# Four gathers, four transposes: one wait per chunk in place of one per transpose

## The chip, the cores and the metric

The kernel runs on one NeuronCore of one Trainium2 chip. The metric is the device time of one execution in microseconds (us), lower is better; where several executions were timed, their median is given. All data is float32.

## What is computed

The reference is the forward pass of a recommendation model. For each of 16384 rows of a batch there are 69 item numbers (fields) and one label number. Each number selects a row of 96 floats from an embedding table of 100001 rows.

```python
u  = emb[batch_user]                         # 16384 x 69 x 96
ql = emb[batch_label[:, 0]]                  # 16384 x 96
z  = concatenate([q, u, q - u, q * u])       # q: ql, repeated for every field
h  = dice(z @ W1 + b1, a1) @ W2 + b2
att = h @ W3 + b3                            # one number per row and field
pre = where(batch_user < ITEM_NUM, u * att, 0)
pooled = einsum('gf,bfe->bge', window, pre)  # 10 groups of fields
x  = concatenate([pooled, ql])
h  = dice(bn(x @ Wf1 + bf1), af1)            # then Wf2, then Wf3
```

`dice(x)` is `(alpha * (1 - p) + p) * x` with `p = sigmoid(x)`. So there are 16384 x 69 = 1.13 million row fetches for the fields, and for each fetched row a small network whose result weights the row in a sum.

## The kernel before, in words

**Tiling.** The batch is cut into 32 blocks of 512 rows (`NBLK`, `BLK`). Of a block, the first 64 fields make 64 chunks of 8 rows x 64 fields, and each of the 5 remaining fields makes a chunk of 512 rows; that is 69 chunks of 512 fetched rows. Two chunks are a pair: 1104 pairs (`NPAIR`), the unit of all loops.

**Fetching.** `fetch(i)` (L298) allots three tiles for pair i: `u` (128 partitions x 8 x 96, from a pool of 14), and the transposed `uT` and `quT`. For each of the two chunks it issues four gathers (L307, which calls `gather`, L226; the profile shows them under L227). A gather is an indirect DMA that GpSimd (POOL) issues: it takes 128 row numbers, one per partition, from the SBUF tile `rows`, and brings 128 table rows of 384 bytes into `u`. After each gather `fetch` records the TensorE transpose of what it brought (L308), into a quarter of the PSUM tile `ptr`. When all four quarters are there, VectorE multiplies `ptr` by the transposed label rows into `quT` (L311, L318), and ScalarE copies `ptr` into `uT` (L319).

**The other stages**, each on an earlier pair: `seed` (L278, a matmul that clears a PSUM bank, and a ScalarE copy into it), `hidden` (L326 the first layer on TensorE; L328 and L329 sigmoid and scaling on ScalarE; L330 the product on VectorE), `attend_rows` (L337, once per four pairs), `spread` (once per four pairs: four transposes L353, then on VectorE L356, and L359, which builds the weights `rw` from two SBUF tiles, `R` and `w`), `pool` (L376, the weighted sum, up to eight matmuls per pair, and L385, its way out), and for the last fields of a block `attend_tail` (L346, L347). Per block there is a top network: `top1` (L406, two halves in four parts each; then L410 on VectorE, L411 and L412 on ScalarE, and L413 on VectorE, a product of two SBUF tiles), `top2` (L420, L421 to L423, and L424, again a product of two SBUF tiles) and `top3` (L429, L431).

**Order.** The order on each engine is written out by hand, in the loop L474 to L507. Step i issues `seed(i-1)`, `pool(i-8)`, every fourth step `attend_rows` or `spread`, `hidden(i-2)`, `fetch(i)`, and after that what the `plan` holds for this step: loads, the gathers of the next block's labels (128 in all, also L227), and one part of the top network. Each engine works through its own queue in this order; the framework adds the semaphore waits that the data needs. A gather into a `u` tile waits for the last matmul of `pool` that read the same tile 14 pairs earlier, and for the gather that used the same one of eight DMA semaphores before.

**Waits in `fetch`.** In the built program [...]a separate event-semaphore instruction with up to two waits stands ahead of it in its engine's queue. The first transpose of a chunk waits for its gather in such an instruction, and for ScalarE (which has to have read the `ptr` tile's earlier contents) in its own. The second, third and fourth each wait for their own gather. In the built program each of the eight transposes of a pair also raises TensorE's semaphore when it is done; VectorE waits for the value of the fourth.

Of the kernel before, what the change touches and what calls it, by code (L numbers as in the profile page):

```python
# [32 lines left out]
I32 = mybir.dt.int32  # L33
AF = mybir.ActivationFunctionType
ALU = mybir.AluOpType
PSUM = bass.MemoryType.PSUM

P = 128
# [25 lines left out]
def rec_kernel(  # L64
# [23 lines left out]
    nc = tc.nc  # L88
# [11 lines left out]
    def load_ids(n):  # L100
        ids = ipool.tile([P, NCOL], I32, tag="ids", name=f"ids{n}")
        nc.sync.dma_start(out=ids, in_=idx[n : n + 1].rearrange("o p n -> (o p) n"))
        return ids

    def map_ids(n, ids):

        rows = ipool.tile([P, NT], I32, tag="rows", name=f"rows{n}")
        nc.vector.scalar_tensor_tensor(rows, ids[:, 0:NT], float(ITEM_NUM), ids[:, 0:NT], ALU.is_ge, ALU.add)
        return rows

    ids, rows = {0: load_ids(0)}, {}
    rows[0] = map_ids(0, ids[0])

    ident = const.tile([P, P], F32, name="ident")
# [16 lines left out]
    for i in range(2):  # L131
        t = const.tile([E + 1, BLK + NS], F32, name=f"qT{i}")
# [10 lines left out]
    def one_minus(t, name):  # L143
        r = const.tile(list(t.shape), F32, name=name)
        nc.vector.tensor_scalar(r, t, -1.0, 1.0, ALU.mult, ALU.add)
        return r
# [43 lines left out]
    for i in range(2):  # L190
        t = const.tile([DH, 1], F32, name=f"sbf1_{i}")
# [7 lines left out]

    with tc.tile_pool(name="prep_ps", bufs=1, space=PSUM) as pps:  # L200
        pv = pps.tile([P, E], F32, name="pv")
# [7 lines left out]

    ps_tr = ctx.enter_context(tc.tile_pool(name="ps_tr", bufs=2, space=PSUM))  # L210
    ps_h = ctx.enter_context(tc.tile_pool(name="ps_h", bufs=2, space=PSUM))
    ps_x = ctx.enter_context(tc.tile_pool(name="ps_x", bufs=2, space=PSUM))
    ps_acc = ctx.enter_context(tc.tile_pool(name="ps_acc", bufs=1, space=PSUM))
    ps_m = ctx.enter_context(tc.tile_pool(name="ps_m", bufs=1, space=PSUM))

# [3 lines left out]
    def tail_weights(f):  # L219
        nc.vector.tensor_scalar_mul(V[:, f, :], wf1[:, 0, :], wr[:, f, 0:1])  # L220
        for g in range(1, G):
            nc.vector.scalar_tensor_tensor(
                V[:, f, :], wf1[:, g, :], wr[:, f, g : g + 1], V[:, f, :], ALU.mult, ALU.add
            )

    def gather(dst, index):  # L226
        nc.gpsimd.indirect_dma_start(  # L227
            out=dst,
            out_offset=None,
            in_=emb,  # L230
            in_offset=bass.IndirectOffsetOnAxis(ap=index, axis=0),
        )

    def chunk(c):

        return divmod(c, NCH)

    def head_gather(n):

        q = bpool.tile([P, NQ, E], F32, tag="q", name=f"q{n}")  # L240
        for k in range(NQ):
            gather(q[:, k, :], ids[n][:, NT + k : NT + k + 1])
        return q
# [27 lines left out]
    def by_field(ap):  # L271

        return ap.rearrange("e (s o) -> e s o", o=1).to_broadcast([ap.shape[0], NS, FM])
# [24 lines left out]
    def fetch(i):  # L298

        u = upool.tile([P, 8, E], F32, tag="u", name=f"u{i}")  # L300
        uT = tpool.tile([E, 2, 512], F32, tag="uT", name=f"uT{i}")
        quT = tpool.tile([E, 2, 512], F32, tag="quT", name=f"quT{i}")
        for j in range(2):
            n, k = chunk(2 * i + j)
            ptr = ps_tr.tile([E, 512], F32, tag="tr", name=f"ptr{i}_{j}")
            for t in range(4):
                gather(u[:, 4 * j + t, :], rows[n][:, 4 * k + t : 4 * k + t + 1])  # L307
                nc.tensor.transpose(ptr[:, t * P : (t + 1) * P], u[:, 4 * j + t, :], ident)  # L308
            q = qTs[n % 2][0:E]
            if k < NMAIN:  # L310
                nc.vector.tensor_tensor(  # L311
                    quT[:, j, :].rearrange("e (s f) -> e s f", f=FM),
                    ptr.rearrange("e (s f) -> e s f", f=FM),
                    by_field(q[:, k * NS : (k + 1) * NS]),
                    ALU.mult,
                )
            else:
                nc.vector.tensor_tensor(quT[:, j, :], ptr, q[:, 0:BLK], ALU.mult)  # L318
            nc.scalar.copy(uT[:, j, :], ptr)  # L319
        return u, uT, quT  # L320
# [21 lines left out]
    def attend_tail(i, j, y, uT):  # L342
# [3 lines left out]
        nc.tensor.matmul(pa, vrep[j * H1 : (j + 1) * H1, :], y[j * H1 : (j + 1) * H1, :], start=True, stop=True)  # L346
        nc.vector.scalar_tensor_tensor(pres[n][:, k - NMAIN, :], pa, bb[0:E], uT[:, j, :], ALU.add, ALU.mult)  # L347

# [121 lines left out]
    with tc.manual_schedule():  # L470
# [3 lines left out]
        for i in range(NPAIR + POOL_LAG + 16):  # L474
            if 0 <= i - 1 < NPAIR:
                phs[i - 1] = seed(i - 1)
            if 0 <= i - POOL_LAG < NPAIR:
                k = i - POOL_LAG
# [6 lines left out]
            if 0 <= i - 3 < NPAIR:  # L485
                k = i - 3
# [11 lines left out]
            if i < NPAIR:  # L498
                for j in range(2):
                    n, k = chunk(2 * i + j)  # L500
                    if n not in pooled:
                        pooled[n] = bpool.tile([E, G, BLK], F32, tag="pooled", name=f"pooled{n}")
                        pres[n] = xpool.tile([E, NTAIL, BLK], F32, tag="pre", name=f"pre{n}")
                u, uT, quT = fetch(i)
                us[i], hs[i] = u, (uT, quT)
# [50 lines left out]
```

## Time and profile before

| what | value |
|---|---|
| median of 7 runs | 11344.1 us (11339.08 to 11354.39) |
| the profiled execution's own time | 11345.01 us |
| its span, first to last instruction | 11343.2 us |
| instructions in the span | 108113 |
| busy: TensorE (PE) / VectorE (DVE) / ScalarE (ACT) / GpSimd (POOL) | 87% / 28% / 33% / 75% |
| mean granted TensorE clock | 0.701 of full speed |
| gathers of fields (L227, `u`) | 8832, mean 952 ns on POOL |
| gathers of labels (L227, `q`) | 128 |
| transposes of gathered rows (L308) | 8832, mean 358 ns |
| from a gather's issue to its landing, median | 2.5 us |

Durations are of one profiled execution, whose own time is 1.8 us above its span. A line of the groups reads: source line, engine, operation, written tile <- read tiles, shape, count, then busy time in all and mean of one, then the idle time of the engine just before these instructions and what ended most of it. "issue" is idle time in which nothing that the profile shows was waited for. In a timeline a row is the start, the duration, then the instruction, and in brackets the idle time before it. The time that POOL is busy with a gather is not the time of the transfer: the transfer goes on after it.

### The profile page before, as it was taken

The numbers are of one execution on the slowest core, as the hardware profiler recorded it, in microseconds if no ns is written. First come the engines' busy times: TensorE is split into PE (matmuls) and PEld (weight loads), VectorE is DVE, ScalarE is ACT, GpSimd is POOL, SyncE is SP. The second block draws the span as 40 slices with busy tenths as digits, with TensorE's granted clock in tenths as the row PEclk, the third lists the DMA queues.
The fourth block names the chain that finished last, engine by engine and source line by source line (L and its number), as shares of the span: only waits on it lengthen the run. The fifth ranks groups of instructions, "written<-read, shape, count | busy, mean of one in ns | idle before, by whom it ended". The sixth has DMA issues, their size and how long they took to land.

```text
span 11343.2 us, 108113 instructions
## 1 busy us (share of the span) xinstructions
PE 9836.0 (87%) x41348; PEld 4774.2 (42%) x41348; DVE 3192.0 (28%) x5424; ACT 3762.4 (33%) x6086; POOL 8531.1 (75%) x8966
## 2 busy tenths in 40 slices
PE   7888888889888888888988888888888888888888
PEld 3444444444444444444444444444444444444444
DVE  3222222222222222222222222222222222222222
ACT  2333333333333333333333333333333333333332
POOL 7777777777777777777777777777777777777775
PEclk6767777666676777766676767677677766767767
DMA  2111111111111111111111111111111111111111
GB/s 44 40 40 40 40 40 40 40 40 40 40 40 40 40 40 40 40 40 40 41 40 40 40 40 40 40 40 40 40 40 40 40 40 40 40 40 40 40 40 29
DMA packets 295008, 453.59 MB, mean 40 GB/s; under 512 B 145952, under 2 KB 151104, under 8 KB 294496
## 3 DMA queue, kind: packets, MB, share of 16 engines
q0 software_dynamic: 286720, 440.98, 18.6%
q8 instruction: 331, 5.42, 0.2%
q1 hardware_dynamic: 6142, 4.77, 0.2%
q14 instruction: 181, 1.48, 0.0%
q10 hardware_dynamic: 1634, 0.94, 0.0%
HBM read 446.04 MB, written 0.07 MB: 39 GB/s over the span
## 4 chain that ended last, share of the span: by engine, by line
POOL 36%; PE 33%; issue 15%; DMA 14%; ACT 2%; DVE 1%; POOLq 0%; ACTq 0%
POOL u L227 34%; DMA u<-in_emb,rows 14%; PE ph L326 11%; PE acc L376 9%; PE p L406 4%; PE ptr L308 3%; PE prow L337 2%; PE ph L278 2%; POOL q L227 1%; PE pa L346 1%; ACT y L329 1%; PE patt L353 1%; DVE y L330 1%; ACT y L328 1%; PE pc L267 0%
## 5 line engine op out<-in xcount | busy, mean ns | idle before, releaser
L227 POOL DMA_INDIRECT u<-in_emb,rows x8832 | 8409.4, 952 | 2691.4 <-issue 2379.0
L308 PE MATMUL ptr<-ident,u 128*96 128x128 f32 x8832 | 2084.9, 358 | 1314.2 <-DMA u<-in_emb,rows 1296.9
L308 PEld LDWEIGHTS ptr<-ident,u 128*96 128x96 f32 x8832 | 1242.1, 157 | 3268.8 <-DMA u<-in_emb,rows 1678.5
L376 PEld LDWEIGHTS acc<-rw,u 128*96 128x96 f32 x16384 | 2066.8, 219 | 495.5 <-issue 494.9
L376 PE MATMUL acc<-rw,u 128*96 128x20 f32 x16384 | 2178.9, 283 | 1.8 <-DVE rw L359 1.3
L319 ACT COPY uT<-ptr 96x512 f32<-96x512 f32 x2208 | 1285.1, 582 | 2321.0 <-DVE quT L311 2137.4
L330 DVE TENSOR_TENSOR y<-ph,y 128x512 f32<-128x512 f32 x1104 | 763.4, 691 | 4455.1 <-ACT y L329 4385.0
L328 ACT ACTIVATE y<-ph 128x512 f32<-128x512 f32 x1104 | 659.4, 597 | 3869.1 <-PE ph L326 3869.0
L326 PE MATMUL ph<-uT,A 96*64 96x512 f32 x4416 | 1821.4, 917 | 0.0
L326 PE MATMUL ph<-quT,w 96*64 96x512 f32 x4416 | 1707.8, 864 | 0.0
L311 DVE TENSOR_TENSOR quT<-ptr,qT 96x512 f32<-96x512 f32 x2048 | 1352.5, 679 | 706.4 <-PE ptr L308 700.9
L385 DVE COPY pooled<-acc 96x160 f32<-96x160 f32 x1008 | 433.4, 430 | 2242.5 <-PE acc L376 2242.0
L326 PEld LDWEIGHTS ph<-quT,w 96*64 96x64 f32 x4416 | 449.5, 197 | 1095.6 <-issue 1095.6
L329 ACT ACTIVATE y<-y,a1c,na1c 128x512 f32<-128x512 f32 x1104 | 897.2, 813 | 37.2
L281 ACT COPY ph<-cT 128x512 f32<-128x512 f32 x1008 | 591.1, 586 | 451.1 <-PE ph L278 449.0
L278 PE MATMUL ph<-zrow 1*128 1x512 bf16 x1104 | 529.8, 480 | 153.7 <-DVE y L330 151.1
L406 PE MATMUL p<-pooled,wf 96*100 96x512 f32 x1280 | 654.1, 655 | 1.2 <-DVE x L410 0.8
L326 PEld LDWEIGHTS ph<-uT,A 96*64 96x64 f32 x4416 | 285.1, 179 | 542.3 <-issue 451.8
L337 PE MATMUL prow<-y,v 128*32 128x512 f32 x2208 | 445.7, 893 | 0.0
L339 ACT COPY row<-prow 128x512 f32<-128x512 f32 x276 | 161.7, 586 | 600.7 <-PE prow L337 599.5
L406 PEld LDWEIGHTS p<-pooled,wf 96*100 96x100 f32 x1280 | 230.4, 189 | 283.0 <-issue 280.7
L406 PE MATMUL p<-pre,V 96*100 96x512 f32 x640 | 311.7, 620 | 0.0
(71 smaller groups left out, 2445.9 us busy)
## 6 DMA issues: line engine op xcount, KB each, us to landing
u<-in_emb,rows POOLq DMA_INDIRECT x8832, 2.5
ids<-in_idx SPq DMA_DIRECT2D x32, 140.0 KB
q<-in_emb,ids POOLq DMA_INDIRECT x128, 2.5
wf<-in_Wf ACTq DMA_DIRECT2D x1, 825.0 KB
out<-res SPq DMA_DIRECT2D x32, 2.0 KB
w<-in_W SPq DMA_DIRECT2D x1, 96.0 KB
wf<-in_Wf ACTq DMA_DIRECT2D x1, 62.5 KB
a1c<-in_a SPq DMA_DIRECT2D x2, 0.2 KB
```

Source lines behind the costliest of these rows:

```text
L227: nc.gpsimd.indirect_dma_start(out=dst, out_offset=None, in_=emb, in_offset=bass.IndirectOffsetOnAxis(ap=index, axis=0),)
L278: nc.tensor.matmul(ph, zrow[:, 0:P], zrow, start=True, stop=False)
L308: nc.tensor.transpose(ptr[:, t * P : (t + 1) * P], u[:, 4 * j + t, :], ident)
L311: nc.vector.tensor_tensor(quT[:, j, :].rearrange("e (s f) -> e s f", f=FM), ptr.rearrange("e (s f) -> e s f", f=FM), by_field(q[:, k * NS ...
L319: nc.scalar.copy(uT[:, j, :], ptr)
L326: nc.tensor.matmul(ph[j * H1 : (j + 1) * H1, :], w, x[:, j, :], start=False, stop=last)
L328: nc.scalar.activation(y, ph, AF.Sigmoid, scale=S_DICE)
L329: nc.scalar.activation(y, y, AF.Identity, bias=a1c, scale=na1c)
L330: nc.vector.tensor_mul(y, ph, y)
L337: nc.tensor.matmul(pr[32 * k : 32 * (k + 1), :], v2, y, start=True, stop=True)
L376: nc.tensor.matmul(pa[:, j, 2 * t : 2 * t + 2, :].rearrange("e n g -> e (n g)"), u[:, 4 * j + t, :], rw[:, i % 4, j, t, :], start=True, st ...
L406: nc.tensor.matmul(p1, w[:, h * DH : (h + 1) * DH], x, start=(k == 0), stop=(k == KTOP - 1))
```

## The change

All eight gathers of a pair are recorded first, chunk 0's four and then chunk 1's four, and after them the transposes. The first transpose of each chunk gets, beside its own, a dependency on the other three gathers of its chunk.

```diff
+SYNC = mybir.DependencyInfo(mybir.DependencyClass.Sync, mybir.DependencyReason.DATA)
...
     def gather(dst, index):
-        nc.gpsimd.indirect_dma_start(
+        return nc.gpsimd.indirect_dma_start(
...
+        sources = []
+        for j in range(2):
+            n, k = chunk(2 * i + j)
+            for t in range(4):
+                sources.append(gather(u[:, 4 * j + t, :], rows[n][:, 4 * k + t : 4 * k + t + 1]))
         for j in range(2):
             n, k = chunk(2 * i + j)
             ptr = ps_tr.tile([E, 512], F32, tag="tr", name=f"ptr{i}_{j}")
             for t in range(4):
-                gather(u[:, 4 * j + t, :], rows[n][:, 4 * k + t : 4 * k + t + 1])
-                nc.tensor.transpose(ptr[:, t * P : (t + 1) * P], u[:, 4 * j + t, :], ident)
+                turn = nc.tensor.transpose(ptr[:, t * P : (t + 1) * P], u[:, 4 * j + t, :], ident)
+                if t == 0:
+
+                    for source in sources[4 * j + 1 : 4 * j + 4]:
+                        tc.add_manual_dep(turn.ins, source.ins.name, SYNC)
```

In the built program, the order of the instructions on every engine stays as it was. POOL's waits and signals are the same, one for one. On TensorE, two event-semaphore instructions with two waits each (four gathers) now stand ahead of the first transpose of a chunk, where there was one with one wait; the other three transposes wait for nothing. Counted over the program, TensorE's event-semaphore instructions go from 2216 to 4426, its matmuls that wait from 11219 to 4595, and those that signal from 13240 to 6616: of a chunk's four transposes the last alone signals, raising the semaphore by four.

## The prediction, made before the changed kernel was run

> **What bounds the kernel now.** I read the page's groups first, then the gather line by itself, then the timeline row by row. POOL looks 75% busy, but its idle time is not waiting:
>
> ```profile
> PE 9836.0 (87%) x41348; PEld 4774.2 (42%) x41348; DVE 3192.0 (28%) x5424; ACT 3762.4 (33%) x6086; POOL 8531.1 (75%) x8966
> ...
> L227 POOL DMA_INDIRECT u<-in_emb,rows x8832 | 8409.4, 952 | 2691.4 <-issue 2379.0
> L308 PE MATMUL ptr<-ident,u 128*96 128x128 f32 x8832 | 2084.9, 358 | 1314.2 <-DMA u<-in_emb,rows 1296.9
> ```
>
> The view of waits gives the longest POOL idle time ahead of a gather, last number of each line, as 0.3 us, whatever releaser it names:
>
> ```profile
> POOL u L227 <- issue: 2379.0, 7807, 0.3
> POOL u L227 <- DMA u<-in_emb,rows: 176.8, 580, 0.3
> POOL u L227 <- PE ptr L308: 117.9, 387, 0.3
> ```
>
> So each gather takes about 0.944 us and 0.305 us of issue, a pitch of 1.249 us, with no pause. The timeline has 8960 gathers (8832 and 128), the first at 3.3 us, the last at 11262.9 us; 8959 pitches in 11259.6 us are 1.257 us each. POOL is the bound until 11263 us; the remaining 80 us are a tail on TensorE. A gather waits for `pool` of 14 pairs before, which TensorE does in step k-6; by the timeline the eighth transpose of a pair started at most 12 us after its gather was issued (median 2.54 us), and a pair is 10 us. TensorE would have to fall some 50 us behind to hold POOL up.
>
> The 1.257 against 1.249 is the only part of POOL's time that can move: 74.0 us, all in 211 gathers that took over 1.0 us. What stretches them shows in the timeline beside VectorE:
>
> ```profile
> 1062.53 0.94 POOL L227 DMA_INDIRECT u<-in_emb,rows  x1 [0.30 <-issue]
> ...
> 1063.70 0.82 DVE L359 TENSOR_TENSOR rw<-R,w 128x640 f32<-128x640 f32 x1
> 1063.78 1.55 POOL L227 DMA_INDIRECT u<-in_emb,rows  x1 [0.30 <-issue]
> ```
>
> L359 started just ahead of the gather, and the gather ends 0.61 us late. The same instruction 0.04 us after a gather's start costs nothing:
>
> ```profile
> 5018.53 0.94 POOL L227 DMA_INDIRECT u<-in_emb,rows  x1 [0.30 <-issue]
> 5018.57 0.82 DVE L359 TENSOR_TENSOR rw<-R,w 128x640 f32<-128x640 f32 x1
> ...
> 5019.77 0.94 POOL L227 DMA_INDIRECT u<-in_emb,rows  x1 [0.30 <-issue]
> ```
>
> And the products of the top network do it too:
>
> ```profile
> 514.41 0.94 POOL L227 DMA_INDIRECT u<-in_emb,rows  x1 [0.30 <-issue]
> ...
> 516.93 0.12 PEld L308 LDWEIGHTS ptr<-ident,u 128*96 128x96 f32 x1 [0.28 <-DMA u<-in_emb,rows]
> ...
> 521.90 0.94 POOL L227 DMA_INDIRECT u<-in_emb,rows  x1 [0.30 <-issue]
> ...
> 523.01 0.69 DVE L413 TENSOR_TENSOR x<-x,g 100x512 f32<-100x512 f32 x1 [1.54 <-ACT g L412]
> 523.15 1.37 POOL L227 DMA_INDIRECT u<-in_emb,rows  x1 [0.30 <-issue]
> ```
>
> Call *phase* the time from the last gather's start to the start of the VectorE instruction, between 0 and 1.249. Over all 276 rows of L359 (0.824 us) and 96 of L413 and L424 (0.69 us) one rule fits: a gather comes to a point 0.123 us after its start at which it is held until the VectorE instruction ends, if that had started by then. So the next gather's stall = phase + duration - (1.249 + 0.123), if positive, for phases under 1.205; above that, none. L359 stalls from phase 0.55 on, up to 0.65 us; L413 and L424 from 0.68, up to 0.52. The rule gives 54.7 us for L359 and 23.8 for the others, 78.5; the records' 74.0 (about 76 with the small ones) make it some 4% generous.
>
> [...] a gather reads its row numbers from SBUF; L359, L413 and L424 have two SBUF inputs; L330 (a PSUM and an SBUF input, 1104 times) stretches none, and 2.7 us of the 74 stay without one of the three beside them.[...] The clock is 0.701 here, and a transpose takes 0.45 or 0.31 us.[...]
>
> **The change part by part.**
>
> *POOL.* Its eight gathers of a pair keep order, waits and signals: 0 us directly. They are recorded ahead of the transposes, but those are in another queue. The waits on `pool` name the same matmul.
>
> *TensorE, removed.* 6624 signals and as many waiting matmuls, less 2210 added event-semaphore instructions. TensorE isn't the bound, so all of it goes into idle time: 0 us.[...]
>
> *TensorE, the wait.* The first transpose now waits for the fourth gather. Behind it in TensorE's queue are the other three, then the plan's work, `seed`, `pool`, `spread`, `hidden`; VectorE and ScalarE wait for these. Before, when the eighth gather lands (2.48 us after issue at best), one transpose is left. After, four are:
>
> ```profile
> 525.26 0.86 PE L308 MATMUL ptr<-ident,u 128*96 128x128 f32 x6
> ...
> 1066.92 1.30 PE L308 MATMUL ptr<-ident,u 128*96 128x128 f32 x5
> ```
>
> Six in 0.86 us at full clock, the last 0.31: (0.86 - 0.31) / 5 = 0.11 apart. Five in 1.30 at half clock, the last 0.45: 0.21 apart. Three more are 0.64 or 0.32 us. The event semaphore: where it stands ahead of a just-landed gather's transpose (the fifth), the start is 2.55 to 2.59 us after issue in the fastest twentieth, against 2.46 to 2.48 without; I take 0.09 us, bounds 0 and 0.3 since two now follow each other. So everything behind the eighth transpose slides by 0.41 us (full clock; bounds 0.3 and 0.7) or 0.73 us (half; 0.6 and 1.0) against the gathers. It doesn't accumulate: 81% of the eighth transposes start within 2.9 us of their gather's issue, so TensorE meets POOL again nearly every pair, and the later ones inherit the slide.
>
> *What the slide does to the stalls.* The three instructions hang on TensorE by fixed chains. L413: 64 times, nearly always at full clock; the eighth transpose starts 2.52 us after its gather's issue, L413 6.08 later: 8.60 - 6 x 1.249 = 1.11, a stall of 0.43 (the row above). After: 1.11 + 0.41 = 1.52, phase 0.27, none. L424: 4.36 behind the transpose, phase 0.6, none; after, 1.01, a stall of 0.33 in some 27 of 32 cases. Together 23.8 becomes 8.9. L359 is spread out. Its 275 instances ahead of the last gather, by phase in quarters (0 to 0.25, to 0.5, 0.75, 1.0, 1.25): full clock at the preceding transpose 47, 19, 45, 55, 24; half clock 15, 6, 9, 20, 35. Moving each by its slide and applying the rule gives 42.9 instead of 54.7. Sum: 51.8 instead of 78.5, 26.7 less; times 0.96, **25.7 us less**. The result depends little on the slide: any from 0.15 to 0.8 us at full clock (half clock 0.3 more) gives 51 to 60.
>
> *Tail.* Of the last pair the eighth transpose is at half clock: +0.7 us on TensorE's chain to the end, once.
>
> Sum: 11345.0 (the profiled execution) - 25.7 + 0.7 = 11320.0. It lies 0.9 above the median, so against the median 11319.
>
> **The rivals.**
>
> 1. *The phases are mixed anew.* TensorE's idle time, until now cut up by single transposes, comes in one piece per chunk[...]. With all phases alike, the rule gives 48.1 for L359 and 10.3 for the rest: 58.4, or 19 us less: 11326.[...]
> 2. *Nothing happens.* If the stretched gathers have another cause that only coincides with VectorE, POOL's 11260 us stay: 11345. Against: the sharp rule over 372 instances.
> 3. *Slower: L359 gathers at the bad phase.* Place: `spread` after a pair met in time at full clock; L359 comes 2.95 us behind the eighth transpose's start, 5.43 after the issue, phase 0.43, no stall. With a slide of 0.41 it is at 0.84, 0.29 us; with 0.75 at 1.18, 0.63 us. If half of the 276 came there at 0.63 (87 us), the others even (138 x 0.18 = 25) and 9 us for the top: 121 instead of 76, 11390. It decides for slower where the mean stall of L359 passes 0.33 us ((76 + 23 - 9) / 276; it is 0.20 now). Against: it needs slide and clock pattern together.
>
> That TensorE falls behind for good would be slower too[...]. But the longest half-clock stretch is 96 us and ended without holding POOL.
>
> **How the numbers follow.** The forecast 0.65 at 11319, own range 11308 to 11331; rival 1 0.19 at 11326 (11316 to 11338); rival 2 0.10 at 11345; rival 3 0.06 at 11390. The range 11304 to 11346 takes in the first three but for their edges. 0.2% (22.7 us, about what a measurement of this kernel can tell from no change) puts the line at 11321: faster 0.65 x 0.7 + 0.19 x 0.4, 0.53; slower 0.06; the rest, 0.41, within.
>
> **What would show it.** Gathers over 1.0 us: about 140 instead of 211, and the mean of L227 949 ns. L413 stretches no gather, L424 most by 0.3. The eighth transpose starts 2.9 to 3.3 us after its gather's issue, four of them 0.11 or 0.21 apart. POOL's idle time ahead of a gather still at most 0.3. It is wrong if gathers still wait 0.3 and stretched ones are as many at other phases (rivals 1, 3), if a gather waits for `acc` (TensorE behind), or if the time moves and the stretched gathers don't.

## The result, and the profile after

The changed kernel takes 11314.1 us (median of 14 runs, 11308.2 to 11323.3) against 11343.6 us for the kernel before (34 runs, 11335.4 to 11354.4): a ratio of 0.9975, interval 0.9968 to 0.9982. It is faster by 0.25%, 29.4 us; 11319 had been predicted. The profiled execution took 11313.2 us, its span is 11311.5 us.

Line numbers have moved: the gather is now L228, the transposes L313, the product into `quT` L320, `rw` L368, the two products of the top network L422 and L433, and the product that makes the row numbers of the next block (L108 before) L109.

The page's engines and the two groups of the change:

```profile
PE 9638.5 (85%) x41348; PEld 4784.1 (42%) x41348; DVE 3186.4 (28%) x5424; ACT 3760.8 (33%) x6086; POOL 8501.5 (75%) x8966
...
L228 POOL DMA_INDIRECT u<-in_emb,rows x8832 | 8379.8, 949 | 2691.6 <-issue 2461.2
L313 PE MATMUL ptr<-ident,u 128*96 128x128 f32 x8832 | 1848.5, 356 | 1442.5 <-DMA u<-in_emb,rows 1382.6
```

TensorE is busy for 197.5 us less, and POOL's idle time ahead of the gathers is the same to 0.2 us. What has moved is the mean of a gather: 949 ns for 952. The view of waits has the same ceiling for POOL as before, 0.3 us in the last number, for `acc` of `pool` too:

```profile
POOL u L228 <- issue: 2461.2, 8076, 0.3
POOL u L228 <- DMA u<-in_emb,rows: 167.9, 551, 0.3
POOL u L228 <- PE ptr L313: 29.6, 97, 0.3
...
POOL u L228 <- PE acc L385: 4.3, 14, 0.3
```

So POOL is still the bound and never waits. The 31.7 us between the two spans add up from the gathers' starts and durations. All gathers over 1.0 us: 211 before, 158 after (about 140 had been forecast); their time above 0.944 us: 74.0 us, now 46.1, that is -27.9. The pitch without this excess: 1.24852 us, now 1.24835, times 8959, -1.5. From the last gather's issue to the end: 80.4 us, now 78.0, -2.4. The first gather: 3.30 us, now 3.44, +0.1.

Which VectorE instruction was running when a gather over 1.0 us was held, taken row by row from the timeline (before and after: gathers, and their time above 0.944 us):

| VectorE instruction | before | after | predicted change | measured |
|---|---|---|---|---|
| `rw`, L359 / L368 | 131, 47.9 | 93, 28.3 | -11.3 | -19.6 |
| top network, L413 and L424 / L422 and L433 | 60, 23.6 | 31, 10.5 | -14.3 | -13.1 |
| near the row numbers, L108 / L109 | 9, 1.2 | 18, 5.3 | 0 | +4.2 |
| the first 130 us | 11, 1.4 | 16, 2.0 | 0 | +0.6 |
| sum | 211, 74.0 | 158, 46.1 | -25.7 | -27.9 |

In the timeline, the same places as before. `rw` in the pair around 1063 us was 0.08 us ahead of a gather; now it begins 0.20 us behind one, and the next gather takes its usual 0.94 us:

```profile
1062.59 0.94 POOL L228 DMA_INDIRECT u<-in_emb,rows  x1 [0.31 <-issue]
1062.79 0.82 DVE L368 TENSOR_TENSOR rw<-R,w 128x640 f32<-128x640 f32 x1
...
1063.83 0.94 POOL L228 DMA_INDIRECT u<-in_emb,rows  x1 [0.30 <-issue]
```

The first product of the top network (L422) now comes at phase 0.26 (869.84 - 869.58), and the transposes of a chunk run four at a time:

```profile
869.58 0.94 POOL L228 DMA_INDIRECT u<-in_emb,rows  x1 [0.30 <-issue]
869.84 0.69 DVE L422 TENSOR_TENSOR x<-x,g 100x512 f32<-100x512 f32 x1 [1.54 <-ACT g L421]
...
870.82 0.94 POOL L228 DMA_INDIRECT u<-in_emb,rows  x1 [0.30 <-issue]
...
871.09 0.64 PE L313 MATMUL ptr<-ident,u 128*96 128x128 f32 x4
...
873.44 1.06 PE L313 MATMUL ptr<-ident,u 128*96 128x128 f32 x4 [1.70 <-DMA u<-in_emb,rows]
```

Four in 0.64 us, the last 0.31: 0.11 us apart at full clock; four in 1.06, the last 0.45: 0.20 at half clock (the records of the granted clock hold two values in both kernels, 1.0 and 0.5). The second product (L433) has come to phase 1.06 and holds the next gather by 0.37 us:

```profile
570.86 0.94 POOL L228 DMA_INDIRECT u<-in_emb,rows  x1 [0.30 <-issue]
...
571.92 0.69 DVE L433 TENSOR_TENSOR x<-x,g 80x512 f32<-80x512 f32 x1 [1.54 <-ACT g L432]
572.11 1.32 POOL L228 DMA_INDIRECT u<-in_emb,rows  x1 [0.30 <-issue]
```

And one thing that the prediction left out, L109, which reads only SBUF and runs once per block:

```profile
2960.96 1.36 POOL L228 DMA_INDIRECT u<-in_emb,rows  x1 [0.30 <-DMA u<-in_emb,rows]
2961.07 0.43 DVE L109 SCALAR_TENSOR_TENSOR rows<-ids 128x276 int32<-128x276 int32 x1
...
2962.62 0.94 POOL L228 DMA_INDIRECT u<-in_emb,rows  x1 [0.30 <-issue]
```

It ended 0.54 us after the gather's start, and the gather was held by 0.41 us. The end fits the prediction's rule (0.54 - 0.12). The start, 0.11 us behind the gather's, does not: no `rw` that began so late held a gather, as the part on the prediction shows.

### The profile page after: what moved, and what is told of

Read it like the earlier page. It is cut to its first block, busy times and chain, and to the rows that moved or that the text cites. A ratio compares the mean times of both kernels' runs of the same rounds, so it can differ in the third digit from the quotient of the medians.

```text
span 11311.5 us, 110323 instructions
## 1 busy us (share of the span) xinstructions
PE 9638.5 (85%) x41348; PEld 4784.1 (42%) x41348; DVE 3186.4 (28%) x5424; ACT 3760.8 (33%) x6086; POOL 8501.5 (75%) x8966
## 4 chain that ended last, share of the span: by engine, by line
POOL 49%; issue 21%; PE 16%; DMA 12%; ACT 1%; DVE 1%; POOLq 0%; ACTq 0%
POOL u L228 49%; DMA u<-in_emb,rows 12%; PE ph L335 5%; PE acc L385 4%; PE p L415 2%; PE ptr L313 1%; PE prow L346 1%; PE ph L279 1%; PE pa L355 1%; ACT y L338 1%; DVE y L339 1%; ACT y L337 1%; POOL q L228 0%; PE patt L362 0%; PE p L438 0%
## 5 line engine op out<-in xcount | busy, mean ns | idle before, releaser
L228 POOL DMA_INDIRECT u<-in_emb,rows x8832 | 8379.8, 949 | 2691.6 <-issue 2461.2
L313 PE MATMUL ptr<-ident,u 128*96 128x128 f32 x8832 | 1848.5, 356 | 1442.5 <-DMA u<-in_emb,rows 1382.6
L313 PEld LDWEIGHTS ptr<-ident,u 128*96 128x96 f32 x8832 | 1199.6, 161 | 3109.0 <-issue 1975.1
L385 PEld LDWEIGHTS acc<-rw,u 128*96 128x96 f32 x16384 | 2102.3, 222 | 541.6 <-issue 540.9
L385 PE MATMUL acc<-rw,u 128*96 128x20 f32 x16384 | 2214.8, 286 | 1.8 <-DVE rw L368 1.3
L320 DVE TENSOR_TENSOR quT<-ptr,qT 96x512 f32<-96x512 f32 x2048 | 1348.8, 679 | 669.5 <-PE ptr L313 665.0
L279 PEld LDWEIGHTS <-zrow 1*128 1x128 bf16 x1104 | 104.4, 95 | 532.8 <-issue 532.8
```

The costliest lines, as they stand in the source:

```text
L228: return nc.gpsimd.indirect_dma_start(out=dst, out_offset=None, in_=emb, in_offset=bass.IndirectOffsetOnAxis(ap=index, axis=0),)
L279: nc.tensor.matmul(ph, zrow[:, 0:P], zrow, start=True, stop=False)
L313: turn = nc.tensor.transpose(ptr[:, t * P : (t + 1) * P], u[:, 4 * j + t, :], ident)
L320: nc.vector.tensor_tensor(quT[:, j, :].rearrange("e (s f) -> e s f", f=FM), ptr.rearrange("e (s f) -> e s f", f=FM), by_field(q[:, k * NS ...
L385: nc.tensor.matmul(pa[:, j, 2 * t : 2 * t + 2, :].rearrange("e n g -> e (n g)"), u[:, 4 * j + t, :], rw[:, i % 4, j, t, :], start=True, st ...
```

## The experiments

**Where they ran.** The theory has two links: (a) a gather is held by a VectorE instruction with two SBUF inputs, by the phase rule; (b) the change slides that work against the gathers, and the slide moves the phases. Rivals: the long gathers only coincide with VectorE, or the gain comes from TensorE's fewer waits and signals. The first ten runs were meant to part them by whole times. They ran on three chips on which the unchanged kernel takes 13415.7, 13575.0 and 13485.8 us, some 19% more than 11343.6. There TensorE stands still again and again (in the trace of the third run, 162 gaps of over 5 us, 1618 us in all), the eighth transpose starts a median 66 us after its gather was issued, and POOL waits for `acc`, the result of `pool`. The view of waits of that run, which changes neither waits nor signals:

```profile
POOL u L227 <- issue: 2206.1, 7226, 0.6
POOL u L227 <- PE acc L377: 763.4, 133, 41.4
```

POOL isn't the bound there, so a whole time there says nothing about POOL's sum. What these traces do tell is what happens to a single gather. The view of them that is used below: of the products that start at least 0.04 us ahead of a gather and still run 0.123 us after its start, the stall that the rule gives in sum (what is *due*), and the one measured. In the two kernels of the result it gives, for `rw`, 49.8 and 48.4 us before (163 products) and 29.4 and 29.0 after (120); one by one, 162 of the 163 and all 120 agree to 0.01 us.

**One PSUM operand in place of the second SBUF operand.** In the kernel before, `w` is kept in unused columns of the PSUM tile `pt`, and the top network's products read their sum from PSUM; its scaling is folded into constants, and L410 and L421 go.

```diff
-        w = rpool.tile([P, 4, 2, 4], F32, tag="w", name=f"w{b}")
+        w = pt[:, 0, :, 2:10]
...
-        nc.vector.tensor_scalar(x1, p1, S_BN, sbf1[h], ALU.mult, ALU.add)
-        nc.scalar.activation(g1, x1, AF.Sigmoid, scale=S_DICE)
+        nc.scalar.activation(g1, p1, AF.Sigmoid, bias=sbf1[h], scale=S_DICE * S_BN)
...
-        nc.vector.tensor_mul(x1, x1, g1)
+        nc.vector.scalar_tensor_tensor(x1, p1, bf1c[h], g1, ALU.add, ALU.mult)
```

> The kernel before, with the three VectorE products of two SBUF tiles reworked so that one operand lies in PSUM: the weights of spread (L359) read w from PSUM, and the products of the top network (L413, L424) read the matmul's result there. Theory (POOL is the bound, and the only part of its time that moves is the stretching of gathers by these three): of the 74 us in stretched gathers some 3 to 5 us are left (start-up, tail weights, row numbers), the tail loses three short instructions (2 us); 11343.5 - 70 - 2 = about 11271, gathers over 1.0 us fewer than 40. Rival A (the gain of the change comes from signals and waits that TensorE no longer has): 11343 to 11341, as nothing of these is touched. Rival B (the stretched gathers have another cause, with which VectorE only coincides): about 11341, and still some 200 gathers over 1.0 us.

Measured: 13378.9 us, ratio 0.9975 (0.9962 to 0.9989) to the kernel before on that chip. The time is no test, for the reason above. The gathers are: 14 of them over 1.0 us, 3.3 us in all, where the kernel before had 211 and 74.0 on the chip of the result. The group of gathers is back at 944 ns:

```profile
L229 POOL DMA_INDIRECT u<-in_emb,rows x8832 | 8335.2, 944 | 4767.8 <-issue 2197.1
```

And it isn't that the products missed the gathers. One that started 0.23 us ahead of a gather, the place where 0.46 us would be due:

```profile
530.65 0.82 DVE L365 TENSOR_TENSOR rw<-R,patt 128x640 f32<-128x640 f32 x1
530.88 0.94 POOL L229 DMA_INDIRECT u<-in_emb,rows  x1 [0.30 <-DMA u<-in_emb,rows]
...
532.13 0.94 POOL L229 DMA_INDIRECT u<-in_emb,rows  x1 [0.30 <-issue]
```

132 products of `rw` lay over a gather's point, due 51.6 us by the rule; measured 0.07 us. Of the first product of the top network 41, due 14.5, measured 0.02. Same instruction, same duration (0.82 us), same place, one operand in PSUM: no stall. That settles link (a) against coincidence.

The same edit in the changed kernel, and both once more on the second chip, and that of the kernel before on the third:

> The changed kernel with the same rework of the three VectorE products. Theory: with nothing left to stretch a gather, the slide of the phases has nothing to act on, so that the change is worth nothing: the same as the reworked kernel before, within 6 us, about 11271. Rival A: the change's 29 us come on top of the rework, 11242. Rival B: about 11312, as the changed kernel.

> The kernel of e1 once more, on a chip on which, it is hoped, the kernel before takes its 11344 us: in e1 to e4 it took 13416, TensorE stood still for 5 to 40 us again and again and was 67 us behind the gathers, so that POOL waited for it and wasn't the bound that all theories here speak of. Theory: POOL bound, 11271, ratio to the kernel before 0.9936, fewer than 40 gathers over 1.0 us (e1 had 14). Rival A (the gain of the change comes from signals and waits that TensorE no longer has): ratio 0.9998 to 1. If TensorE stands still again: 0.9975 as in e1.

> The kernel of e2 once more, for the same reason. Theory: the change is worth nothing where nothing stretches a gather: the time of e5 within 6 us, about 11271, ratio 0.9936. Rival A: 29 us less than e5, 11242, ratio 0.991.

> The kernel of e1 and e5 a third time. Where POOL is the bound: 11271, ratio 0.9936, fewer than 40 gathers over 1.0 us (e1 had 14). Rival A: ratio 0.9998 to 1. Where TensorE stands still: 0.9975 to 1.0014, as in e1 and e5.

Measured, in this order: 13390.8 us (ratio 0.9973, 0.996 to 0.9985), 13607.4 (1.0014, 0.9994 to 1.0034), 13680.7 (1.0075, 1.0045 to 1.0104), 13533.9 (1.0028, 1.0013 to 1.0042). The sign of the same edit differs from chip to chip, so these times tell nothing on the change. The gathers agree everywhere: 14, 9, 11 and 11 over 1.0 us, 2.2 to 3.8 us in all, while 130 to 151 products of `rw` were due 45 to 54 us and cost 0.3.

**The fourth gather's transpose first.** The kernel before with a chunk's gathers recorded first and its transposes in the order 4, 1, 2, 3; all waits and signals stay. The three transposes behind can't start before the last gather has landed, as in the change. It parts the slide from the saved waits and signals.

```diff
             for t in range(4):
                 gather(u[:, 4 * j + t, :], rows[n][:, 4 * k + t : 4 * k + t + 1])
+            for t in (3, 0, 1, 2):
                 nc.tensor.transpose(ptr[:, t * P : (t + 1) * P], u[:, 4 * j + t, :], ident)
```

> The kernel before, every wait and signal kept (13240 signalling matmuls, 11219 waiting ones), but in each chunk the transpose of the fourth gather stands first and the other three behind it, so that they too run only when the fourth has landed. Theory: this is the slide of 0.4 (full clock) or 0.7 us (half clock) without the removal, so the gain is that of the change: 11309 to 11322, L413 at phase 0.2 to 0.35 and stretching nothing, L424 at about 1.0. Rival A: nothing was removed, 11343.

> The kernel of e3 once more. Theory: every wait and signal of the kernel before is kept, but the transposes run when the fourth gather has landed; the slide alone brings the gain of the change: 11309 to 11322, ratio 0.997 to 0.998. Rival A: ratio 1.

> The kernel of e3 and e7 a third time. On both chips so far TensorE stood still again and again and POOL waited for it, for the kernel before too. Where POOL is the bound (the kernel before at 11344), the theory says: the slide alone, with every wait and signal kept, brings the change's gain, 11309 to 11322, ratio 0.997 to 0.998, no gather stretched by L413. Rival A (removed waits and signals): ratio 1. Where TensorE stands still: ratio 1, as in e3 and e7.

Measured: 13408.3 us (0.9997, 0.9979 to 1.0014), 13580.5 (1.0, 0.9982 to 1.0018), 13481.9 (0.9991, 0.9979 to 1.0003): no difference, on chips where TensorE is 66 us late and a slide of half a microsecond has nothing to act on. In the third run 2 of the 1104 eighth transposes started within 3.6 us of their gather's issue, where 77% did in the changed kernel. Inconclusive on the time. On link (a) they count: with two SBUF operands, 173, 156 and 185 gathers are over 1.0 us, and the rule holds on these chips too: `rw` is due 54.6, 42.1 and 47.0 us and cost 54.4, 41.8 and 46.5.

**The change, with `rw` put 0.2 us later** by one more VectorE instruction ahead of it, which writes a quarter of `w` again:

```diff
+        nc.vector.tensor_scalar(w[:, :, :, 0], pt[:, 0, :, 0:2], bb, None, ALU.add)
         nc.vector.tensor_tensor(
             rw.rearrange("p k j t g -> p k (j t) g"),
```

> The changed kernel with one more short VectorE instruction between L356 and L359 of the line numbers before (it writes eight of the 32 numbers of w once more), so that the weights of spread begin about 0.22 us later against the gathers, and nothing else moves. Theory: the rule for the stall, applied to the 276 phases in the changed kernel's trace, gives 59 to 62 us in place of 33 for a shift of 0.20 to 0.25 us (56 at 0.15 and 0.28), so 23 to 29 us slower: 11337 to 11343, all of the change's gain lost again through VectorE's phase alone. Rival A: 11314, since TensorE's waits and signals are those of the changed kernel and VectorE has 70% idle time.

> The kernel of e4 once more: the changed kernel with the weights of spread about 0.22 us later on VectorE. Theory: 23 to 29 us slower than the changed kernel, 11337 to 11343, ratio 0.9994 to 1; stretched gathers by L359 59 to 62 us in place of 33. Rival A: ratio 0.9975, as the changed kernel.

Measured: 13368.2 us (0.9966, 0.9953 to 0.9978) and 13624.7 (1.003, 1.0015 to 1.0045), again of both signs: no finding on the time. The stalls of `rw` are 24.2 us (24.4 by the rule) and 32.5 (33.1).

The gathers recorded ahead of the transposes without the joint wait were not run: that is the kernel before, instruction for instruction. The three bare transposes without the joint wait would be a race and weren't tried.

**Gathers alone, with the product at a chosen phase.** All else left out (the output is zeros): the 8832 gathers, and from the second of 16 stretches of 69 pairs on, a small VectorE instruction that waits for a pair's last gather, copies as a pause, and a product of the size of `rw`. The pause grows from stretch to stretch; in the second stretch the product reads a PSUM operand.

```diff
+            nc.vector.tensor_tensor(s, u[:, 7, 0:1], quiet[:, 0:1], ALU.mult)
+            pause(i, step)
+            product(i, W)
```

> The disputed cost by itself; all of the model but the gathers is left out, and the output is zeros. The 8832 gathers of u in the order of the kernel before, and no TensorE at all, so that a chip on which TensorE stands still tells nothing else. The 1104 pairs fall into 16 stretches of 69. In the first VectorE does nothing. In the others one short VectorE instruction waits for the eighth gather of the pair, one or two copies out of PSUM follow as a pause, and then comes the product of L359 (128 x 640, 0.82 us): in the second stretch with one operand in PSUM, in the other fourteen with both in SBUF, with pauses that put its start at phases of about 0.20, 0.37, 0.47, 0.57, 0.67, 0.77, 0.87, 0.96, 1.01, 1.06, 1.11, 1.16, 0.01 and 0.11 us. Theory: the first stretch runs at 1.248 us a gather (689 us), no pause of POOL: gathers alone fill 11.03 ms; the product with a PSUM operand stretches none; the others stretch one gather per pair by phase - 0.55 up to phase 1.2 and by nothing after it: 0, 0, 0, 0.02, 0.12, 0.22, 0.32, 0.41, 0.46, 0.51, 0.56, 0.61, 0, 0 us. Sum 3.23 x 69 = 223 us, the kernel 11.25 ms. Rival B (another cause, VectorE only coincides): no stretch follows the phase; if any VectorE work did it, the PSUM stretch would show 0.5 us a pair too.

Measured: 12369.7 us, and the expected total of 11.25 ms is missed. The stalls are not. By stretch, the median phase, the median stall, and what the rule gives for this duration (phase + 0.816 - 1.372), in us:

| phase | 0.14 to 0.50 (five stretches) | 0.641 | 0.703 | 0.745 | 0.815 | 0.914 | 0.988 | 1.080 | 0.770, PSUM operand |
|---|---|---|---|---|---|---|---|---|---|
| stall | 0.00 | 0.082 | 0.143 | 0.185 | 0.250 | 0.355 | 0.427 | 0.515 | 0.00 |
| rule | 0 | 0.085 | 0.147 | 0.189 | 0.259 | 0.358 | 0.432 | 0.524 | (0.214) |

Two more stretches, at phases 0.725 and 0.830, gave 0.165 and 0.272 us (rule 0.169 and 0.274). Two rows each of the timeline, first the last stretch, then the one with the PSUM operand:

```profile
11908.38 0.81 DVE L140 TENSOR_TENSOR rw<-R,W 128x640 f32<-128x640 f32 x1
11908.51 1.50 POOL L126 DMA_INDIRECT u<-in_emb,rows  x1 [0.30 <-DMA u<-in_emb,rows]
```

```profile
1099.25 0.81 DVE L140 TENSOR_TENSOR rw<-R,quiet 128x640 f32<-128x640 f32 x1
1099.64 0.94 POOL L126 DMA_INDIRECT u<-in_emb,rows  x1 [0.30 <-issue]
```

The total is missed because something else held POOL on that chip: from 237 us on, still without any VectorE work, gathers come 1.400 us apart.

```profile
405.45 1.09 POOL L126 DMA_INDIRECT u<-in_emb,rows  x1 [0.30 <-issue]
406.85 1.09 POOL L126 DMA_INDIRECT u<-in_emb,rows  x1 [0.30 <-issue]
```

Every later stretch takes 771 to 774 us, whatever its stalls, and 552 gathers at 1.400 us are 772.8: the stalls are absorbed in this slower pace. In the kernels of the result there is no such pace (1.248 us, above).

**Gathers and transposes in three orders.** Six stretches of 184 pairs: each transpose behind its own gather; one joint wait per chunk; the fourth first. Behind them a pause and the product; the rest left out (the output is zeros).

```diff
+                for s, t in enumerate((3, 0, 1, 2) if style == "fourth" else range(4)):
+                    turn = nc.tensor.transpose(ptr[:, t * P : (t + 1) * P], u[:, 4 * j + t, :], ident)
+                    if style == "joint" and s == 0:
+                        for source in sources[1:]:
+                            tc.add_manual_dep(turn.ins, source.ins.name, SYNC)
```

> The slide by itself; left out is all but the gathers, their transposes, and per pair one copy out of ptr as a pause and one product as in L359; the output is zeros.[...] Six stretches of 184 pairs: with a pause of about 0.5 us the transposes as before (each waits for its own gather), as changed (the first waits for all four, the others neither wait nor signal), and with the fourth gather's transpose first and all waits and signals kept; then the same three with a pause of about 1.05 us. Theory: the product comes at phase 1.0 before and 1.73 - 1.25 = 0.48 in the two others, so a stretch of 0.45 us a pair (83 us) in the first and none in the second and third; with the longer pause at 1.52 - 1.25 = 0.27 before, and at 1.0 in the two others: none, 0.45, 0.40 to 0.45. So the change gains in one half and loses as much in the other, and the third order does as the second. Rival A (removed waits and signals are the gain): the changed order is the faster in both halves, and the third order equals the first.

Measured: 12500.5 us, missed: TensorE is late here too (median 70 to 80 us), and the stretches take 2050 to 2105 us in no order. But some pairs, 25 to 34 of each stretch, met their gathers in time. At the fifth percentile of a stretch the eighth transpose starts so long after its gather's issue: own waits 2.51 us in both stretches, joint wait 3.24 and 3.21, fourth first 3.24 and 3.26, at half clock (mean granted clock of the run 0.54). The slide is 0.73 us, and keeping every wait and signal gives the same slide as dropping them. So in these pairs it is where the transposes are queued that slides the work, not the number of waits and signals. In the pairs that were in time, the stall per pair with the shorter pause is 0.35 us (own), 0.09 (joint) and 0.06 (fourth first), with the longer one 0.02, 0.15 and 0.27; the phases' rule gives 0.33, 0.09, 0.06 and 0.03, 0.21, 0.30. The same slide takes stalls away or adds them, depending on where the product stood before.

## Why the prediction was right, and where it was not

- *What bounds.* Right: POOL goes from the first gather to the last without a wait in both kernels (idle for at most 0.3 us ahead of any), and what moved is the time of stretched gathers. 27.9 of the 31.7 us of the spans are theirs.
- *The cause of the stretch.* Right, and shown: with one operand in PSUM, 132 products due 51.6 us cost 0.07; with two in SBUF, `rw` held gathers by up to 0.65 us (the longest took 1.60 us). L330, which has one operand in PSUM, lay over a gather's point in the same way 453 times in the kernel before, and none of these gathers took over 0.95 us. Which part of a gather is held isn't shown.
- *The rule's border.* In words, the prediction has a gather held by whatever has started by 0.123 us after the gather's start. In the traces of the two kernels the border lies earlier, and it is sharp. The 222 products before and 155 after (`rw` and the top network's two) that began at least 0.045 us ahead of a gather, and ran past 0.123 us after its start, each held it for the time due, to within 0.01 us. Of the 56 and 38 that began later, from 0.044 us ahead of a gather's start to 0.123 us behind it, none held it. The sums used phases under 1.205, which is 0.044 us ahead of the next gather, so they stand; the 0.123 tells only how long a stall is. Close to the border it is the product that waits: 23 of `rw` before and 12 after began between 0.044 us ahead of a gather and 0.025 us behind it. They took 0.83 to 0.90 us in place of 0.82, and all ended 0.85 to 0.86 us after the gather's start. With an operand in PSUM (first run), 19 of `rw` in the same place took 0.82 us as ever. One row of each kernel, with its gather:

```profile
4817.72 0.89 DVE L359 TENSOR_TENSOR rw<-R,w 128x640 f32<-128x640 f32 x1
4817.75 0.94 POOL L227 DMA_INDIRECT u<-in_emb,rows  x1 [0.30 <-issue]
```

```profile
2041.97 0.82 DVE L365 TENSOR_TENSOR rw<-R,patt 128x640 f32<-128x640 f32 x1
2042.00 0.94 POOL L229 DMA_INDIRECT u<-in_emb,rows  x1 [0.30 <-issue]
```

- *The slide.* Right to 0.02 us. The medians of the eighth transpose after its gather's issue: 2.54 before; after, 2.97 at full clock and 3.28 at half clock, slides of 0.43 and 0.74, predicted 0.41 and 0.73. Within 2.9 us: 81% before, 4% after; within 3.6 us, 77% after, so TensorE still meets POOL in most pairs.
- *The top network.* L413's stalls were to vanish and did but for 4 of 64 (1.2 us); L424's were to become 0.33 us in some 27 of 32 and are 27, 9.3 us in all. 13.1 us less, predicted 14.3.
- *`rw`: the term that was mis-sized.* 42.9 us was predicted by moving each instance by its slide; the same rule over the phases that came gives 33.3. At half clock it was right (10.3 predicted, 10.2); the full clock was off (32.5, 23.2). There 44 instances were to be at a phase over 1.0, and 17 were. Moving each instance takes its clock for granted, and 86 of 275 had the other clock after the change: rival 1's mixing of the phases, partly at work. But that is only half of the miss: the 189 that kept their clock come to 27.7 us by the move and 23.0 by the phases that came, the other 86 to 15.3 and 10.3. The step that was off is that `rw` hangs on TensorE by a fixed chain. In the kernel before, the top network's L413 started 6.08 us behind the last eighth transpose in most cases, but `rw` anywhere from 2.9 to 7.0 us (tenth to ninetieth percentile). And of the 189, only 88 slid by the predicted amount to within 0.15 us, where pure chance would give some 45. What else moves `rw`, and how much is the chance of one execution, isn't settled; 275 independent stalls of the spread measured after would scatter by 3.1 us.
- *The rule's own size.* Counted by phase alone it is 14% too high for `rw` before (54.7 by the rule, 47.9 in gathers over 1.0 us), not 4%: a stretched gather starts the next one later, which the fixed pitch of 1.249 leaves out. Of the excess, 5.7 us lie at places where the gather ahead of the product was itself stretched. Counted against the gathers' true starts the rule gives 49.8 for a measured 48.4.
- *Left out.* The row numbers (L109) were not in the sum and took 4.2 us back. Of the 18 gathers there, one fits the rule in full. Seven were held until L109 had ended, as the rule has it, although it began 0.05 to 0.15 us after their start; in each of the seven it stood directly behind a product into `quT` that was still running when the gather started. These eight are 3.0 us. The other ten were held by 0.15 to 0.27 us, although L109 began 0.37 us or more after their start. Neither is explained.
- *Tail.* +0.7 us was predicted, -2.4 came. The mean granted clock in these last 80 us was 0.69 before and 0.76 after; the prediction took the clock to stay. (Nor is the longest stretch at half clock before 96 us: by the clock's records it is 75, which does not touch the sum.)
- *TensorE's saved signals and waits.* Right at 0 us: TensorE's busy time is 197.5 us less, and POOL's idle time is the same to 0.2 us.

That the sum comes within 5 us is partly luck, two errors of opposite sign: `rw` 8.3 us better than predicted, the row numbers 4.2 worse.

Open: no chip on which POOL is the bound was had again. So neither the slide alone (the fourth gather's transpose first) nor the kernel before without the products of two SBUF tiles was timed where it counts; that the slide brings the gain rests on the sums above and on the few pairs of the last run. By the sums the kernel before without these products would take some 11270 us (11343.6 - 74.0, and some 3 us left as in the first run), and the change would then be worth nothing but its tail. That is an estimate, from the excess of the gathers alone.

## What to carry over

When an engine is the bound and never waits, look at the spread of one of its instructions, not at its waits: 2% of the gathers held nearly all the time that moved. A change that only slides work can pay or cost through whom it runs beside, and the sign depends on the phase: in the last run the joint wait took the stall per pair from 0.35 to 0.09 us with the shorter pause, and from 0.02 to 0.15 with the longer. So its gain is measured for this schedule alone. One operand in PSUM removed the stretch at all phases that came up: 0.07 us were left where 51.6 were due.

## What the runs showed of the hardware

- The same program takes 11344 us in one place and 13416 to 13575 us on three chips. On these the data of gathers still lands in time (in the third run the last packet of a gather ends about 2.1 us after its issue), but TensorE stands still for up to 35 us at a time in that run, and its signals come in bursts: eight within 0.3 us after 18 us of none. Most records of DMA semaphores are missing in these traces, so where the signals are held isn't seen. The cause stays open.
- Gathers alone, with nothing beside them, ran at 1.249 us for some 190 gathers and then at 1.400 us on one of these chips, POOL busy 1.09 us for each in place of 0.94.
- Between a gather and a floating-point product of two SBUF tiles, in the two kernels of the result, one of the two waits. A product that began at least 0.045 us ahead of the gather's start, and ran past 0.123 us after it, held it until the product ended: 222 before and 155 after, for the time due to within 0.01 us, up to 0.65 us. Those that began later, 56 and 38 of them up to 0.123 us behind the start, cost the gather nothing; nor did they in the run of the gathers alone, where the product ran beside 0.8 us of a gather (phase 0.14, stall 0.00). One that began from 0.044 us ahead to 0.025 us behind was itself held, by up to 0.075 us (`rw`, 23 and 12). With one operand in PSUM neither held the other (132 products: 0.07 us in all; 19 of `rw` by the border: 0.82 us each). The row numbers (L109, integers) don't keep to this border, and why stays open.
